# Two chunks of a shared expert behind the routed experts, as seven products of quarters

## The chip, the core and the metric

The kernel runs on one core of one Trainium2 chip, in float32. The metric is the device time of one execution in microseconds (us), from runs of the whole program. A profile is one execution recorded by the hardware; its times count from the span's start.

## What is computed

Input are x (4 batches of 1024 tokens with 1024 channels), a side input of the same size, and weights. Two layers follow each other.

```python
mix(r, k) = sigmoid(r) * num / max(den, 1e-8) * (0.8 + 0.2*tf)   # num, den: forward and backward scans over time
x = x + mix(x, f) @ (w0 * s0).T + b0                              # layer 0
x = x + moe(mix(x, f))                                            # layer 1
# moe(y): h = rmsnorm(y) * nw
#   routed: each token's 4 best of 32 experts, silu(h @ w1[:, :512]) * (h @ w1[:, 512:]) @ w2, weighted sum
#   shared: (silu(h @ sg) * (h @ su)) @ sd,  sg, su, sd of 1024 x 1024
#   result: y + routed + shared
```

The part that matters here is the shared expert: three products of 1024 x 1024 matrices for each of 4096 tokens.

## The kernel before

The tokens are cut into 8 chunks of 512 (q = 0 to 7, two to a batch). A chunk stands in the memory as 8 tiles of 128 channels x 512 tokens. A product of a 1024 x 1024 matrix with a chunk is 8 pieces (one for each 128 output channels); a piece is 8 matmuls of 128 x 128 by 128 x 512 that gather in one bank of PSUM.

**First stage.** VectorE mixes: 64 units, one for each batch, tile of 128 channels and layer; the last three batches hold layer 0 and layer 1 of each tile beside each other. A unit is a forward scan of two halves (L281), a backward scan (L293), and passes (L324, L325, L311, L312, L314 and L315 for layer 0, L317 for layer 1), spread over three steps. ACT does the exponentials and stores a finished unit with a DMA in its own queue (L341). TensorE runs pieces: `first_ffn(q)` (L433, layer 0 of a chunk, then the gate of layer 1 in L467 and its residual in `resT_d`), `shared_up(q)` (L645, 16 pieces: gate and up of the shared expert in turn, L654 multiplies) and `shared_down(q)` (L673, 8 pieces, each followed by 4 transposes in L678 and a store into `sum_d`). `norm_route(q)` (L525 to L616) normalises, chooses the experts and writes rows of h for the experts' gathers.

The order of TensorE's pieces is written out in `order()` (L895 to L921). The order of VectorE against them is planned while the program is built: `run` keeps an account of VectorE's and TensorE's work in microseconds and writes out mixing steps while VectorE's account is below `PACE` (0.9) times TensorE's. Evacuations of a piece are written out one or two pieces later (`after`). `mix_until` writes out all mixing steps that a piece's inputs need. Each engine then runs its own list in order and waits where data are not there. Loads are issued on SP's queue in the order of the list, two pieces ahead; a load that waits holds up those behind it.

The end of that order before:

```python
for b in range(2, B):
    q = NCH * b
    pieces += first_ffn(q, True) + first_ffn(q + 1, True) + shared_down(q - 1)
    pieces += shared_up(q) + shared_down(q)
    if b + 1 < B:
        pieces += shared_up(q + 1)
```

So chunk 7 alone has no shared expert here. During the last 32 pieces the plan of the experts is made (`plan`) and their first weights come in.

**Experts.** 68 units of two blocks of 128 tokens and 12 of one block. A unit of two does its products in the manner of Strassen and Winograd: a product of two matrices cut into quarters takes seven products of quarters instead of eight, and 4 sums of each side and 7 of results. `products` (L1109 to L1152) is that sequence: seven products in three PSUM banks, ACT copies the first, VectorE adds the others. VectorE makes the sums of weights (L838, L858) and of tokens (L984 to L988). Results are added to rows of `sum_d` by an indirect DMA (L1101).

**Tail.** Behind the last unit stands the shared expert of chunk 7: 16 pieces (L1305) with silu and multiplication (L1309, L1310), then 8 pieces (L1329) with bias and residual (L1334). Each 128 x 512 result is turned by 4 transposes (L1315), added to the rows that hold the experts' sums (L1317) and stored (L1318). Its h was kept in `hT_d` by `norm_route(7)` (L530) and is loaded while the last units run (`ahead_1`, `ahead_2`). Seven copies bring the finished chunks from `sum_d` to the output (L1285).

Of the kernel before, what the change touches and what calls it, by code (L numbers as in the profile page):

```python
# [8 lines left out]
FP = mybir.dt.float32  # L9
# [3 lines left out]
ALU = mybir.AluOpType  # L13
# [9 lines left out]
P = 128  # L23
# [8 lines left out]
def kernel(  # L32
# [37 lines left out]

    c0_d = dram.tile([B, NC, P, T], FP, name="c0_d")
    c1_d = dram.tile([B, NC, P, T], FP, name="c1_d")
    hT_d = dram.tile([NC, P, CH], FP, name="hT_d")
    resT_d = dram.tile([NC, P, NT], FP, name="resT_d")

    h_d = dram.tile([NT + P, C], FP, name="h_d")
# [75 lines left out]
    with tc.tile_pool(name="empty", bufs=1) as pz:  # L152
        zeros = pz.tile([P, 2 * C], FP, name="zeros")
        nc.gpsimd.memset(zeros, 0.0)
        nc.sync.dma_start(out=h_d[bass.ts(NT // P, P), :], in_=zeros[:, 0:C])
        nil_i = pz.tile([P, E * BPE // P, BLK], I32, name="nil_i")
        nc.gpsimd.iota(nil_i, pattern=[[0, E * BPE // P], [1, BLK]], base=NT, channel_multiplier=0)
        nil = pz.tile([P, E * BPE // P, BLK, 2], FP, name="nil")
        nc.gpsimd.memset(nil, 0.0)
        nc.gpsimd.tensor_copy(nil[:, :, :, 0], nil_i)  # L160
        nc.sync.dma_start(
            out=slots_d[0 : E * BPE * BLK, :].rearrange("(p r s) o -> p r s o", p=P, s=BLK), in_=nil
        )
        nc.sync.dma_start(
            out=slots_d[E * BPE * BLK :, :].rearrange("(p s) o -> p s o", p=1), in_=nil[0:1, 0, :, :]
        )

        for n in range((NT - CH) // P, NT // P, 2):
            nc.scalar.dma_start(
                out=sum_d[bass.ds(n * P, 2 * P), :].rearrange("(p r) c -> p (r c)", p=P), in_=zeros  # L170
            )
        nc.scalar.dma_start(out=sum_d[bass.ts(NT // P, P), :], in_=zeros[:, 0:C])
# [37 lines left out]
    W_SCANS, W_MIN, W_PASS, W_HALF = 4.7, 0.7, 1.25, 0.75  # L210
    W_PIECE, W_SMALL = 6.9, 1.0
    LATENCY = 12.0
    PACE = 0.9
    table = [None]

    def exp_ln(to, of, func, **kw):
# [152 lines left out]

    beside = []  # L370
    c1s, rTs = {}, {}

    class Piece:

# [29 lines left out]
    def first_ffn(q, gated):  # L404
# [4 lines left out]
        def early(ot):  # L409
            if not gated:  # L410

                nc.sync.dma_start(out=resT_d[ot, :, bass.ts(q, CH)], in_=xT[b, bass.ts(ot, P), cols])
            else:
                xs[ot] = px.tile([P, CH], FP, name="x")
                nc.sync.dma_start(out=xs[ot], in_=xT[b, bass.ts(ot, P), cols])
            if ot == 0:
                mix_until(*((b, ct, 0) for ct in range(NC)))
                if q == 0:
                    work["tensor"] += LATENCY
                for ct in range(NC):  # L420
                    c0s.append(pc0.tile([P, CH], FP, name="c0"))
                    nc.sync.dma_start(out=c0s[ct], in_=c0_d[b, ct, :, cols])
            tiles[ot] = pw0.tile([P, NC, P], FP, name="w0t")
            nc.sync.dma_start(out=tiles[ot], in_=w0[ot])
            if gated:
                mix_until((b, ot, 1))
                c1s[q, ot] = (ph, pc1)[q % NCH].tile([P, CH], FP, name="c1")
                nc.sync.dma_start(out=c1s[q, ot], in_=c1_d[b, ot, :, cols])

        def do(ot):  # L430
# [87 lines left out]
    def norm_route(q):  # L518
# [7 lines left out]
        yield 3.4, 0.0  # L526
        for ct in range(NC):
            nc.vector.scalar_tensor_tensor(hs[ct], hs[ct], v["nw"][:, ct : ct + 1], rs, ALU.mult, ALU.mult)
            if q == NT // CH - 1:
                nc.sync.dma_start(out=hT_d[ct], in_=hs[ct])  # L530
        yield NC * W_HALF, 0.0
        lgT_ps = ps_tr.tile([E, CH], FP, name="tr")
        for ct in range(NC):
# [361 lines left out]
    def order():  # L895
# [18 lines left out]
        pieces += first_ffn(2, True) + first_ffn(3, True) + shared_up(2) + shared_down(2) + shared_up(3)  # L914
        for b in range(2, B):
            q = NCH * b
            pieces += first_ffn(q, True) + first_ffn(q + 1, True) + shared_down(q - 1)
            pieces += shared_up(q) + shared_down(q)
            if b + 1 < B:
                pieces += shared_up(q + 1)  # L920
        return pieces  # L921

    with tc.manual_schedule(engines={PE, DVE, ACT, POOL, SP}):
# [13 lines left out]
    with ExitStack() as m:  # L937
# [220 lines left out]
            for _ in s:  # L1158
                pass

        def run_units(us, loaded, ahead=()):


            if not loaded:
# [40 lines left out]
                held = u  # L1205
            rest_of(held.left)
            rest_of(held.down_sums)
            rest_of(held.down())
            held.add()

# [29 lines left out]

        last = NT // CH - 1
        cols = bass.ts(last, CH)
        end = {}

        def pieces_of(tile):
            flat = tile.rearrange("p k f -> p (k f)")
            n = flat.shape[1] // C
            return [flat[:, bass.ts(i, C)].rearrange("p (k f) -> p k f", f=P) for i in range(n)]  # L1250

        def weights(i):

            to = end["places"][i % len(end["places"])]
            f, n = divmod(i, 2)
            w = (sg, su)[n][:, bass.ts(f, P)] if f < NSI else sd[:, bass.ts(i - 2 * NSI, P)]
            nc.sync.dma_start(out=to, in_=w.rearrange("(k p) f -> p k f", p=P))
            return to

        before_last, last_unit = (len(whole) - 2) % 2, (len(whole) - 1) % 2  # L1260

        def ahead_1():
            one, two = have["w1"][before_last]
            hT = end["hT"] = one.rearrange("p k (h t) -> p (k h) t", t=CH)
            nc.sync.dma_start(out=hT, in_=hT_d.rearrange("k p t -> p k t"))
            end["places"] = pieces_of(two)
            end["wt"] = {i: weights(i) for i in range(4)}

        def ahead_2():
            end["places"] = end["places"] + [x for w in have["w1"][last_unit] for x in pieces_of(w)]  # L1270
            for i in range(4, 12):
                end["wt"][i] = weights(i)

        main = [Unit(u, i % 2) for i, u in enumerate(whole)]
        with tc.manual_schedule(engines=ENG):
# [1 line left out]
                u.load = iter(())  # L1277
            main[0].up_sums = iter(())
            main[0].hs = have["first"]
            run_units(main, True, (ahead_1, ahead_2))  # L1280

            o = have["w2"][before_last]
            nc.sync.dma_start(out=o, in_=sum_d[bass.ts(last, CH), :].rearrange("(t p) c -> p t c", p=P))
            for q in range(last):
                nc.sync.dma_start(out=out[bass.ts(q, CH), :], in_=sum_d[bass.ts(q, CH), :])  # L1285
            acts = [have["t_up"][i][:, k, :] for i in (2, 3) for k in range(NK)]
            rs = [have["t_up"][4][:, k, :] for k in range(NK)]
            banks = [(ps_g, "gA"), (ps_g, "gB"), (ps_g, "gC"), (ps_y, "dA"), (ps_y, "dB"), (ps_y, "dC")]
            used = 0

            def bank():
                nonlocal used
                pool, name = banks[used % len(banks)]
                used += 1
                return pool.tile([P, CH], FP, name=name)

            wt, hT = end["wt"], end["hT"]
            lead = len(end["places"])
            for f in range(NSI):
                gu = []  # L1300
                for n in range(2):
                    i = 2 * f + n
                    mm = bank()
                    for kt in range(NC):
                        nc.tensor.matmul(mm, lhsT=wt[i][:, kt, :], rhs=hT[:, kt, :], start=(kt == 0), stop=(kt == NC - 1))  # L1305
                    gu.append(mm)
                    if i + lead < 2 * NSI + NC:
                        wt[i + lead] = weights(i + lead)
                nc.scalar.activation(acts[f], gu[0], AF.Silu)  # L1309
                nc.vector.tensor_tensor(acts[f], acts[f], gu[1], ALU.mult)  # L1310

            def turned(ct, r):
                rows = ps_t.tile([P, CH // P, P], FP, name="tr")
                for t in range(CH // P):
                    nc.tensor.transpose(rows[:, t, :], r[:, bass.ts(t, P)], ident)  # L1315
                part_o = o[:, :, bass.ts(ct, P)]
                nc.vector.tensor_tensor(part_o, part_o, rows, ALU.add)  # L1317
                nc.scalar.dma_start(  # L1318
                    out=out[cols, bass.ts(ct, P)].rearrange("(t p) c -> p t c", p=P), in_=part_o
                )  # L1320

            held = None
            for ct in range(NC):
                i = 2 * NSI + ct
                r = rs[ct % len(rs)]
                nc.sync.dma_start(out=r, in_=resT_d[ct, :, cols])
                mm = bank()
                for f in range(NSI):
                    nc.tensor.matmul(mm, lhsT=wt[i][:, f, :], rhs=acts[f], start=(f == 0), stop=(f == NSI - 1))  # L1329
                if i + lead < 2 * NSI + NC:  # L1330
                    wt[i + lead] = weights(i + lead)
                if held:
                    turned(*held)
                nc.vector.scalar_tensor_tensor(r, mm, v["b0"][:, ct : ct + 1], r, ALU.add, ALU.add)  # L1334
                held = (ct, r)
            turned(*held)


# [55 lines left out]
```

## Time and profile before

Three runs took 5104.92, 5109.55 and 5104.85 us, median 5104.92. The profiled execution took 5109.81 us with a span of 5107.8 us.

| stretch of the span (us) | what runs | TensorE busy | VectorE busy |
|---|---|---|---|
| 0 to 197 | mixing alone | 0 | nearly full |
| 400 to 1150 | mixing beside pieces | 740.9 of 750 | 625.8 |
| 1150 to 1465 | chunks 4 and 5, mixing of batch 3 | 306.4 of 315 | 255.1 |
| 1465 to 1633 | down of 4, up of 5 | 168.0 of 168 | 32.6 |
| 1633 to 2022 | chunks 6 and 7, routing, plan | nearly full | light |
| 2022 to 4934 | experts | full | about half |
| 4934 to 5108 | shared expert of chunk 7 | nearly full | light |

The profile's columns: engine, line of the kernel, operation, output and inputs, count; in a timeline the first two numbers are start and duration in us, and brackets give the idle time before it and what ended that. PE is TensorE's matmul, PEld its weight load, DVE VectorE, ACT ScalarE, POOL GpSimd, SP the engine that issues loads. A float32 matmul appears as two passes, so 8 matmuls count x16. Matmul durations overlap; the distance of starts is their pace.

### The profile page before, as it was taken

To read this page: it belongs to the slowest core of one execution; us is meant where nothing else is said; L and a number is where in the kernel's file an instruction comes from. 1 tells how busy PE (TensorE), PEld (TensorE's weight loads), DVE (VectorE), ACT (ScalarE), POOL (GpSimd) and SP (SyncE) were. 2 spreads that over 40 slices of the span, in tenths; PEclk is the share of its full clock that TensorE was granted. 3 is DMA by queue.
4 is the path that set the end of the run, shared out by engine and by line. 5 is a ranking of instruction groups with operands and counts; after the bars stand their busy time and mean duration, and the time that the engine had idled before them with its cause. 6 is when DMAs were issued, how large, how long until landed. Compare 5 with 4: busy or idle time off the path is not lost.

```text
span 5107.8 us, 36503 instructions
## 1 busy us (share of the span) xinstructions
PE 4823.9 (94%) x12906; PEld 2235.0 (44%) x12906; DVE 3130.7 (61%) x3280; ACT 1445.5 (28%) x1840; POOL 818.4 (16%) x765
## 2 busy tenths in 40 slices
PE   0479999999999998999999999999999999999999
PEld 0124444444444443444444444444444444444444
DVE  9988887887860222656565656556565656565621
ACT  5557656566540210111111111111111111111110
POOL 0113202302310220111111111111111111111110
PEclk9989999999999999999999999999999999999999
DMA  4678679669754845676767676767676777777784
GB/s 139 192 206 216 181 222 269 174 198 277 194 160 127 236 128 189 214 233 220 233 216 241 212 241 212 241 214 239 214 239 214 239 229 224 229 224 229 224 233 118
DMA packets 524212, 1077.77 MB, mean 211 GB/s; under 512 B 30642, under 2 KB 260147, under 8 KB 523411
## 3 DMA queue, kind: packets, MB, share of 16 engines
q1 hardware_dynamic: 386338, 744.70, 42.9%
q0 software_dynamic: 74656, 223.12, 20.9%
q10 hardware_dynamic: 63024, 107.50, 6.0%
q8 instruction: 105, 1.72, 0.1%
q14 instruction: 89, 0.72, 0.0%
HBM read 844.13 MB, written 203.56 MB: 205 GB/s over the span
## 4 chain that ended last, share of the span: by engine, by line
PE 60%; ACT 0%; issue 0%; DVE 0%; ACTq 0%
PE gA L1117 14%; PE gC L1117 9%; PE gB L1117 9%; PE dA L1117 7%; PE dB L1117 5%; PE dC L1117 5%; PE tr L971 2%; PE gA L1005 2%; PE gB L1005 2%; PE tr L1054 1%; PE dA L1067 1%; PE dB L1067 1%; PE gB L1305 0%; PE gC L1305 0%; PE gA L1305 0%; PE dA L1305 0%
## 5 line engine op out<-in xcount | busy, mean ns | idle before, releaser
L645 PE MATMUL mm<-c,wpc 128*128 128x512 f32 x1792 | 777.7, 593 | 0.9 <-DMA wpc<-in_su 0.9
L433 PE MATMUL mm<-c,w0t 128*128 128x512 f32 x1024 | 447.9, 599 | 213.9 <-DMA w0t<-in_w 212.4
L645 PEld LDWEIGHTS mm<-c,wpc 128*128 128x128 f32 x1792 | 337.9, 190 | 416.1 <-issue 412.5
L1117 PE MATMUL gA<-w,hsT 128*128 128x512 f32 x1088 | 489.6, 593 | 0.0
L1117 PE MATMUL gC<-w,s_up 128*128 128x512 f32 x1088 | 489.1, 592 | 0.0
L1117 PE MATMUL gB<-t_up,s_up 128*128 128x512 f32 x1088 | 489.1, 592 | 0.0
L1101 POOL DMA_INDIRECT sum_d<-y,tokens x148 | 306.3, 2070 | 917.2 <-DMA sum_d<-y,tokens 541.8
L871 POOL DMA_INDIRECT hs<-h_d,tokens x146 | 147.7, 1012 | 1621.8 <-PE tr L971 1540.3
L433 PEld LDWEIGHTS mm<-c,w0t 128*128 128x128 f32 x1024 | 196.2, 192 | 461.8 <-issue 456.4
L673 PE MATMUL mm<-sact,wpc 128*128 128x512 f32 x896 | 395.2, 596 | 0.0
L1117 PEld LDWEIGHTS gB<-t_up,s_up 128*128 128x128 f32 x1088 | 206.7, 190 | 260.2 <-issue 244.2
L1117 PEld LDWEIGHTS gC<-w,s_up 128*128 128x128 f32 x1088 | 206.7, 190 | 260.2 <-issue 260.2
L838 DVE TENSOR_TENSOR t_up<-w,w 128x2048 f32<-128x2048 f32 x136 | 310.7, 2285 | 0.0
L1117 PEld LDWEIGHTS gA<-w,hsT 128*128 128x128 f32 x1088 | 201.7, 190 | 227.8 <-issue 227.8
L293 DVE TENSOR_TENSOR_SCAN fg<-decay,tail,fg 128x1024 f32<-128x1024 f32 x128 | 292.9, 2330 | 0.0
L1117 PE MATMUL dB<-t_down,s_down 128*128 128x512 f32 x544 | 256.9, 595 | 0.1
L1117 PE MATMUL dA<-w,actT 128*128 128x512 f32 x544 | 255.8, 592 | 0.0
L1117 PE MATMUL dC<-w,s_down 128*128 128x512 f32 x544 | 255.8, 592 | 0.0
L972 ACT COPY hsT<-tr 128x512 f32<-128x512 f32 x296 | 172.7, 588 | 291.8 <-PE tr L971 291.8
L673 PEld LDWEIGHTS mm<-sact,wpc 128*128 128x128 f32 x896 | 168.1, 191 | 198.2 <-issue 196.7
L1117 PE MATMUL gA<-t_up,hsT 128*128 128x512 f32 x544 | 244.5, 592 | 0.0
L1042 ACT ACTIVATE act<-c 128x512 f32<-128x512 f32 x68 | 42.8, 630 | 708.9 <-DVE c L1038 708.9
(245 smaller groups left out, 6210.8 us busy)
## 6 DMA issues: line engine op xcount, KB each, us to landing
w<-in_w SPq DMA_DIRECT2D x240, 2048.0 KB, 9.1
fg<-euk POOLq DMA_DIRECT2D x64, 512.0 KB, 6.5
c_d<-r ACTq DMA_DIRECT2D x64, 512.0 KB, 7.9
c<-c_d SPq DMA_DIRECT2D x128, 256.0 KB, 6.8
w0t<-in_w SPq DMA_DIRECT2D x64, 512.0 KB, 6.4
wpc<-in_sg SPq DMA_DIRECT2D x56, 512.0 KB, 5.0
wpc<-in_su SPq DMA_DIRECT2D x56, 512.0 KB, 5.0
wpc<-in_sd SPq DMA_DIRECT2D x56, 512.0 KB, 5.4
```

The source lines that it names most:

```text
L293: nc.vector.tensor_tensor_scan(fg[:, m, ::-1], decay[L][:, ct, b : b + 1].to_broadcast([P, T]), fg[:, m, ::-1], tail[:, m : m + 1], ALU.mu ...
L433: nc.tensor.matmul(mm, lhsT=tiles[ot][:, it, :], rhs=c0s[it], start=(it == 0), stop=(it == NC - 1))
L645: nc.tensor.matmul(mm, lhsT=wts[f, n][:, kt, :], rhs=c1s[q, kt], start=(kt == 0), stop=(kt == NC - 1))
L673: nc.tensor.matmul(mm, lhsT=wts[ct][:, f, :], rhs=acts[q, f], start=(f == 0), stop=(f == NSI - 1))
L838: nc.vector.tensor_tensor(to, x, y, ALU.subtract)
L871: nc.gpsimd.indirect_dma_start(out=to, out_offset=None, in_=h_d, in_offset=bass.IndirectOffsetOnAxis(ap=have["tokens"][:, i, n : n + 1], a ...
L971: nc.tensor.transpose(tr[:, r, :], hs[:, bass.ts(4 * q + r, P)], ident)
L972: nc.scalar.copy(self.hsT[:, 4 * q : 4 * q + 4, b, :], tr)
L1005: nc.tensor.matmul(ps, lhsT=self.hsT[:, k, 0, :], rhs=w[k // NK][:, k % NK, bass.ts(n, I)], start=(k == 0), stop=(k == NC - 1),)
L1067: nc.tensor.matmul(ps, lhsT=self.actT[:, k, 0, :], rhs=w[:, k, bass.ts(n, 512)], start=(k == 0), stop=(k == NI - 1),)
L1101: nc.gpsimd.indirect_dma_start(out=sum_d, out_offset=bass.IndirectOffsetOnAxis(ap=tokens[:, i, self.n : self.n + 1], axis=0), in_=y, in_of ...
L1117: nc.tensor.matmul(ps, lhsT=x[:, k, :], rhs=w[:, k, :], start=(k == 0 and not more), stop=(k == half - 1), skip_group_check=more,)
```

## The change

The shared expert of chunk 6 leaves the first stage, and stands with that of chunk 7 in the tail, where the two chunks side by side (1024 tokens) are multiplied in seven products of quarters. The order becomes:

```diff
-            pieces += first_ffn(q, True) + first_ffn(q + 1, True) + shared_down(q - 1)
-            pieces += shared_up(q) + shared_down(q)
+            pieces += first_ffn(q, True) + first_ffn(q + 1, True)
             if b + 1 < B:
-                pieces += shared_up(q + 1)
+                pieces += shared_down(q - 1) + shared_up(q)
+            else:
+                pieces += shared_down(q - 2) + shared_up(q - 1) + shared_down(q - 1)
```

Ahead of chunk 6's first layer 24 pieces are gone (down of 4, up of 5), and the 32 behind chunk 7 are down of 4, up of 5, down of 5. Since chunk 5's tiles are still held then, chunk 7's gate tiles lie in two buffers of the mixing (`fg`). `PACE` becomes 0.93. `hT_d` holds two chunks, so chunk 6's h is stored too (8 DMAs more on SP's queue), and the zeros for `sum_d` cover one chunk more (two DMAs of 1 MB more on ACT's queue at the start).

The tail is new. `weights(i)` loads two tiles of 128 columns, one of each half of the matrix; unit i of 0 to 7 is gate or up (in turn) of output tiles m and m + 4, units 8 to 11 are down. Each unit makes four sums of its weights, and seven products of four matmuls:

```diff
+        def weight_sums(i):
...
+            nc.vector.tensor_tensor(s[1], a21, a22, ALU.add)
+            nc.vector.tensor_tensor(s[2], s[1], a11, ALU.subtract)
+            yield
+            nc.vector.tensor_tensor(s[3], a11, a21, ALU.subtract)
+            nc.vector.tensor_tensor(s[4], a12, s[2], ALU.subtract)
+            yield
...
+        def chunk_sums(quarters, t):
+            (b11, b12), (b21, b22) = quarters
+            for to, x, y in ((t[3], b22, b12), (b12, b12, b11), (t[2], b22, b12), (t[4], b21, t[2])):
+                nc.vector.tensor_tensor(to, x, y, ALU.subtract)
+                yield
...
+            for i in range(NSI):
+                m = i // 2
+                if 0 < i and i + 3 < NSI + HF:
+                    weights(i + 3)
+                nxt = weight_sums(i + 1)
+                take = take_up(m) if i % 2 else take_gate(m)
+                for n, _ in enumerate(unit_of(i, h_quarters, have["t_up"], HF, take)):
+                    if n < 4:
+                        next(done, None)
+                    elif n < 6:
+                        next(nxt, None)
+                rest_of(done)
+                rest_of(nxt)
+                done = act_sums(m) if i % 2 else iter(())
+                if i < tail:
+                    nc.sync.dma_start(out=out[bass.ts(i, CH), :], in_=sum_d[bass.ts(i, CH), :])
```

The sums of the two chunks' h (four of 128 x 2048) are made once, in `begin_tail`, which `run_units` calls behind the last token sums and ahead of the last unit's down product; the sums of the activations (four of 128 x 512) are made after each up unit. `take_gate` and `take_up` add, apply silu and multiply per quarter. The four down units add bias and residual and turn each result as before, 16 in all. The first weights go to token buffers and to the weights of the last unit of two; three units ahead are under way at a time. The copies to the output are six, one after each of the first six units.

## The prediction

> **What bounds the kernel now.** First the page's shares of busy time and its slices:
>
> ```profile
> PE 4823.9 (94%) x12906; PEld 2235.0 (44%) x12906; DVE 3130.7 (61%) x3280; ACT 1445.5 (28%) x1840; POOL 818.4 (16%) x765
> PE   0479999999999998999999999999999999999999
> DVE  9988887887860222656565656556565656565621
> ```
>
> From the fourth slice TensorE (PE) is busy nearly throughout; VectorE (DVE) is near full only in the first twelve slices, where the mixing runs beside the matmuls. Two places matter: the end of the mixing, where the change takes matmuls away, and the tail, where it puts them back. The first, in TensorE's timeline (start, length; each matmul shows as two passes):
>
> ```profile
> 1150.29 55.10 PE L433 MATMUL mm<-c,w0t 128*128 128x512 f32 x128
> 1213.50 43.49 PE L433 MATMUL mm<-c,w0t 128*128 128x512 f32 x96 [8.11 <-DMA w0t<-in_w]
> ...
> 1464.78 20.76 PE L673 MATMUL mm<-sact,wpc 128*128 128x512 f32 x48
> ...
> 1633.10 55.10 PE L433 MATMUL mm<-c,w0t 128*128 128x512 f32 x128
> ```
>
> 1150.29 is the first layer's product of chunk 4, 1633.10 that of chunk 6. At 1464.78 the up products of chunk 4 are over; from there to 1633.10 stand the 24 pieces that the change takes out of this place. When the mixing ends, in VectorE's timeline:
>
> ```profile
> 1465.05 0.69 DVE L654 TENSOR_TENSOR sact<-sact,mm 128x512 f32<-128x512 f32 x1 [8.33 <-PE mm L645]
> ...
> 1482.67 1.23 DVE L315 TENSOR_TENSOR r<-r,xg 128x1024 f32<-128x1024 f32 x1 [1.50 <-ACT xg L224]
> ...
> 1493.57 1.23 DVE L317 TENSOR_TENSOR r<-r,fg 128x1024 f32<-128x1024 f32 x1 [0.52 <-DMA fg<-euk]
> ```
>
> L315 at 1482.67 finishes the last layer-0 unit of batch 3, which chunk 6 needs; L317 the last of all. VectorE here waits for TensorE (8.33 us before L654): the mixing ends at 1494 because its steps stand behind products, not because VectorE is full. Last the tail:
>
> ```profile
> 4933.53 7.03 PE L1305 MATMUL gA<-w,w 128*128 128x512 f32 x16
> ...
> 5057.13 0.60 PE L1315 MATMUL tr<-ident,t_up 128*128 128x128 f32 x4
> 5057.57 7.03 PE L1329 MATMUL gA<-t_up,w 128*128 128x512 f32 x16
> ...
> 5100.97 0.60 PE L1315 MATMUL tr<-ident,t_up 128*128 128x128 f32 x4
> 5103.10 0.63 PE L1315 MATMUL tr<-ident,t_up 128*128 128x128 f32 x4 [1.53 <-DVE t_up L1334]
> ```
>
> From 4933.53 the 24 pieces of chunk 7 follow each other every 6.87 us without a gap; the last ends at 5100.97, and 6.83 us later the span is over.
>
> **The change, part by part.** A piece is 8 matmuls and takes 6.867 us from start to start, so one matmul 0.858 us. A group of four transposes takes 0.44.
>
> *Taken from the first stage:* 1633.10 - 1464.78 = 168.3 us (24 x 6.867 = 164.8, and 8 transpose groups, 3.5). What follows chunk 7's first layer keeps its shape, 8 down, 16 up and 8 down pieces (of chunks 4 and 5 in place of 5 and 6), so routing and plan have the same cover of 32 pieces.
>
> *Put into the tail:* 8 up and 4 down units of 7 products of 4 matmuls: 336 matmuls, where the two chunks took 384. 336 x 0.858 = 288.4; 15 of the 16 transpose groups on the path, 6.6; the end as now with one more VectorE add ahead of it, 6.83 + 0.69 = 7.5. Tail 302.5, before 174.3 (4933.53 to the span's end 5107.8): +128.2.
>
> [...] The row decides: pieces start exactly 6.87 us apart with the next one's operands there, so 48 x 0.858 = 41.2 us go.
>
> *Does the mixing end in time?* Without the 24 pieces chunk 6 could begin at 1464.8. In the new order on VectorE the last layer-0 unit of batch 3 stands behind the product of the fifth gate (L654's place) of chunk 4, the last layer-1 unit behind the sixth; in the old one they stand behind the first and second down piece after the next chunk's up. The fifth product ends six pieces before 1464.8, at 1423.6. Then L654 0.7, two scans 4.5, four passes 4.9: 1433.7. In the trace the store of the 1482.67 result is issued at 1489.48, 5.6 us after its end, and such stores land in 5.3 to 9.2 us: 1444.6 to 1448.5. The load on SP takes 6.6 to 8.7, with the weight tile close behind it: 1452 to 1458. That is 7 to 13 us before 1464.8, so no wait, if VectorE keeps up. From the first product of chunk 4 (1157.2) to the fifth gate it has 20 forward and 20 backward scans (2.3 us each), eleven units' L324 and L325 (2.4 a unit), ten units' L311 and L312 (2.4), L314 with L315 (2.5) or L317 (1.2), 9 of new keys, 61 half passes of 0.74, two reciprocals of 3.4 and 11 of routing: some 234 us in 266, 88%. In this stretch it now runs at 255 of 315 (81%), in its fullest 50 us at 47.05 (94%). It must also have come 1.7 units (some 28 us) further by 1157, which the planner's 0.93 in place of 0.9 asks of it; between 400 and 1150 it was idle for 124 of 750 us. So it keeps up with little to spare: I take 0, bounds 0 and +37 (mixing as late as now: data at 1502). A gain is excluded, since the pieces are already counted out in full.
>
> *Small edits at nothing, and their cover.* Two more 1 MB stores of zeros on ACT's queue at 10 us: ACT idles 9.65 us after, and the next k load, issued at 21.31, is needed at 34.04, when 5 us more of traffic (390 to 420 GB/s there) have passed; without cover up to 5. Eight more stores of normed rows on SP wait for VectorE's norm, with the down weights queued behind; chunk 7 does this now with no gap on TensorE; up to 5. Chunk 6's gate tiles now wait on SP until the last up piece of chunk 4 has used its tiles, with the second weight tile (6.7 us to land) queued behind; the wait ends 6 us before chunk 6 begins and the tile is needed 6.87 us after it. Six copies of sums to the output, one per unit, for seven at once, and 1 MB of weights per 24 us, asked for three units ahead: some 5 MB per 24 us, 210 GB/s, where the tail now moves 340 in its fullest 50 us.
>
> *The new chain into the tail.* VectorE is free at 4926.1 (last y). Two weight sums of 0.69 and three chunk sums of 2.29 (the L838 row, 128x2048) put the third sum's result at 4934.4; the second product needs it at 4933.5 + 3.4 = 4937.0. The chunks' loads start at 4879 and 4886, the first weights at about 4899. Covered by 2.6 us; without cover the whole 12 us of sums. I take 1.
>
> *VectorE inside the tail.* Of 24.0 us per unit a gate takes 9 operations of 0.69, an up unit 17, a down unit 13 and four of 0.75: 6 to 12 us. The experts' stage runs this same helper with 0.0 idle before its matmuls. Taken as 0, upper bound one 1.4 us handover per unit, 17; below nothing is excluded.
>
> Sum: -168.3 + 128.2 + 1 = -39.1. The profiled execution took 5109.8 us (span 5107.8 and 2.0 around it), giving 5070.7. It lies 4.9 above the median 5104.92 and next to the highest of the three; against the median the sum gives 5066.
>
> **Rivals.**
> 1. *The mixing comes late* and TensorE waits at chunk 6, by 10 to 37 us: 5076 to 5103, say 5088. For it: VectorE's 88%, and routing steps that wait up to 9.9 us for small products. Against: the 7 to 13 us of margin. 8%.
> 2. *Handovers in the tail show*, up to 17 us, or the 12 us of first sums: about 5080. Against: the experts' 0.0. 7%.
> 3. *Slower.* Place: chunk 6's first product; mechanism: with the 24 pieces gone, the same mixing has to fit in 168 us less matmul time, and VectorE becomes the bound there. The gain is gone when the wait passes 39 us, and it is slower by 0.2% (about what a measurement can tell from no change, 10 us) from a wait of 49: the last layer-0 unit would have to end after 1494, later than now, so VectorE would do its 234 us in 327, 72%, under the 81% it shows. Priced at 55 us: 5121. 3%.
> 4. *The matmuls are not saved* because products of four need more time each than pieces of eight: the order shows 336 in place of 384, and the experts' products of 8 passes start 3.43 us apart, the same 0.43 per pass. [...] 2%.
>
> **How the numbers follow.** The forecast's own case, 80%, is 5066 with 5058 to 5075 around it (the 4.9 us between the runs, small edits up to 5). 8 in 10 would be met by that; since the upper ends of rivals 1 and 2 are real I reach to 5088. Faster by over 0.2% (below 5094.7) takes the forecast's case, rivals 2 and 4 and half or more of 1: 0.93. Within 0.2%: the late part of 1, 0.04. Slower: 0.03.
>
> **What would show it.** Right: chunk 6's first product starts near 1465 with no wait on c loads; the experts start near 1854 in place of 2022.42; the tail is about 302 us with products 3.43 us apart. Wrong: a wait before chunk 6's products or a gap between products in the tail. The prediction falls if VectorE lags behind the products of chunks 4 and 5, and the waits there are for VectorE.

## The result and the profile after

| | before | after |
|---|---|---|
| median of 20 runs each | 5106.49 us (5101.79 to 5111.55) | 5095.67 us (5090.31 to 5104.23) |
| ratio | 1 | 0.998, 95% interval 0.9973 to 0.9987 |
| profiled execution, span | 5109.81, 5107.8 us | 5095.89, 5093.8 us |

The kernel became 0.2% faster: 10.8 us by the medians, a little over a quarter of the 39 us that the prediction summed up. In the changed kernel the lines of the first stage stand some 7 lower down: L433 is now L440, L645 L652, L673 L680, L678 L685, L819 L826. The page after, busy time first and then the slices:

```profile
PE 4793.8 (94%) x12810; PEld 2220.2 (44%) x12810; DVE 3225.9 (63%) x3416; ACT 1434.3 (28%) x1833; POOL 811.1 (16%) x765
PE   0479999999899979999999999999999999999999
DVE  9988988888752226565656565565656565656434
```

TensorE's busy time is 30 us less, but the span only 14 us shorter. In TensorE's row the eleventh slice (1273 to 1401 us) is now 8, where it was 9, and the one in which the experts begin is 7, where it was 8. TensorE's timeline at the same places as in the prediction, with its new waits between them:

```profile
1150.46 55.10 PE L440 MATMUL mm<-c,w0t 128*128 128x512 f32 x128
1209.09 43.13 PE L440 MATMUL mm<-c,w0t 128*128 128x512 f32 x96 [3.53 <-DMA w0t<-in_w]
...
1302.16 1.12 PE L685 MATMUL tr<-ident,rT 128*128 128x128 f32 x4 [6.17 <-ACT hr L554]
1306.97 1.12 PE L552 MATMUL tr<-ident,c 128*128 128x128 f32 x4 [2.71 <-ACT rT L686]
...
1377.72 1.11 PE L552 MATMUL tr<-ident,c 128*128 128x128 f32 x4 [4.71 <-ACT rT L686]
...
1478.77 55.10 PE L440 MATMUL mm<-c,w0t 128*128 128x512 f32 x128
...
1807.39 8.69 PE L680 MATMUL mm<-sact,wpc 128*128 128x512 f32 x16 [12.18 <-DMA wpc<-in_sd]
...
1881.22 3.78 PE L980 MATMUL tr<-ident,t_down 128*128 128x128 f32 x16 [11.46 <-DVEq L1243]
...
4792.48 3.60 PE L1126 MATMUL gA<-w,hs 128*128 128x512 f32 x8
...
5088.84 0.63 PE L1461 MATMUL tr<-ident,t_up 128*128 128x128 f32 x4 [1.22 <-DVE t_up L1475]
```

The waits of 3.53 and 11.46 us are not new (8.11 and 11.59 before). Read the rest by stretches. The tail (4792.48 to 5093.8) is 301.3 us, the experts (1881.22 to 4792.48) 2911.3 as before (2911.1). Chunk 6's first product begins at 1478.77, not 1465, and the experts at 1881.22, not 1854. So all 27 us that are missing lie ahead of the experts: the stretch from chunk 4's first product to the end of its up products grew from 314.5 to 328.3 (+13.8), and that from chunk 6's first product to the experts from 389.3 to 402.5 (+13.1).

**Loss one, ahead of chunk 6.** There is no wait for chunk 6's data at 1478.77. TensorE waits earlier, in the routing of chunks 4 and 5, and for ScalarE. ScalarE's timeline after:

```profile
1267.27 0.71 ACT L224 ACTIVATE y<-x,v_b 128x512 f32<-128x512 f32 x1
1280.70 0.57 ACT L543 COPY hr<-tr 32x512 f32<-32x512 f32 x1 [12.73 <-PE tr L541]
1281.30 1.28 ACT L219 ACT_TABLE_LOAD   x1
1282.59 1.06 ACT L220 ACTIVATE ek<-ek 128x1024 f32<-128x1024 f32 x1
...
1297.23 1.06 ACT L224 ACTIVATE xg<-xg 128x1024 f32<-128x1024 f32 x1 [4.40 <-DMA xg<-in_xT]
...
1301.54 0.56 ACT L554 COPY hr<-tr 128x512 f32<-128x512 f32 x1
```

and VectorE's:

```profile
1267.52 0.68 DVE L253 TENSOR_SCALAR ek<-k 128x1024 f32<-128x1024 f32 x1
...
1270.63 1.22 DVE L317 TENSOR_TENSOR r<-r,fg 128x1024 f32<-128x1024 f32 x1
1283.68 1.23 DVE L259 TENSOR_TENSOR ekv<-ek,k 128x1024 f32<-128x1024 f32 x1 [11.82 <-ACT ek L220]
```

VectorE has the input of the exponential `ek` ready at 1268.2. ScalarE does `ek` at 1282.59, because in its queue `ek` stands behind the copy of chunk 4's router logits (L543), and that copy waits 12.73 us for logits whose matmuls (L541) stand on TensorE behind a product. VectorE idles 11.82 us for `ek`; the mixing steps are then late, and with them what ScalarE does for them. One of these, the sigmoid of `xg`, waits 4.40 us more for its load, which ScalarE issued only behind the late exponentials. Behind all of this stand the copies of turned rows (L554 at 1301.54), whose PSUM banks TensorE needs at 1302.16. So a wait for TensorE came back to TensorE by way of two other queues. In the kernel before the same copy waited 11.07 us, and no `ek` stood behind it:

```profile
1285.47 0.57 ACT L536 COPY hr<-tr 32x512 f32<-32x512 f32 x1 [11.07 <-PE tr L534]
...
1286.35 1.06 ACT L224 ACTIVATE xg<-xg 128x1024 f32<-128x1024 f32 x1 [0.30 <-issue]
```

Nothing passed the waiting copy: ScalarE ran nothing from 1267.98 to 1280.70, and `ek` came 14.4 us after its input.

The windows' view of the stretch from the end of chunk 5's first layer to the end of chunk 4's up products (length; busy PE, PEld, DVE, ACT, POOL; granted clock, DMA share, GB/s), before:

```profile
1271.40:1464.80 193.40, 192.92 (x532) 87.99 (x531) 158.69 (x169) 111.81 (x118) 60.94 (x78) 1.00 0.66 178
```

and after:

```profile
1266.70:1478.80 212.10, 198.27 (x532) 90.45 (x531) 154.41 (x168) 109.44 (x116) 61.74 (x81) 0.96 0.68 185
```

The same 532 matmuls took 18.7 us more: TensorE's idle time grew from 0.5 to 13.8 us, and 5.4 us went to slower matmuls (busy 198.27 for 192.92), with a granted clock of 0.96 in place of 1.00 (the four transposes after each wait take 1.12 us where they take 0.66 elsewhere). VectorE was busy 154 of 212 us, 73%: it was not full. The stall at 1209.09, ahead of this stretch, gave 4.6 us back (3.53 in place of 8.11).

**Loss two, behind chunk 7's first layer.** SP's timeline (issues of loads) after:

```profile
1771.82 0.37 SPq L673 DMA_DIRECT2D wpc<-in_sd  x1
1787.05 1.00 SPq L826 DMA_DIRECT2D w<-in_w  x2
1788.09 0.51 SPq L673 DMA_DIRECT2D wpc<-in_sd  x1
1788.79 12.65 SPq L833 DMA_DIRECT2D w<-in_w  x1
1801.48 0.51 SPq L673 DMA_DIRECT2D wpc<-in_sd  x1
```

and its waits there (in total, times, longest):

```profile
SPq L826 <- PE mm L652: 13.5, 1, 13.5
```

Before, the same load was issued 1.7 us behind the first tile of down weights:

```profile
1925.59 0.37 SPq L666 DMA_DIRECT2D wpc<-in_sd  x1
1927.27 0.97 SPq L819 DMA_DIRECT2D w<-in_w  x2
```

L826 (L819 before) loads the first expert's weights. The tiles stand where the stack of pools was that `plan` closes, and one of those pools, `pc1`, holds chunk 5. Before, the up products in this place were chunk 6's, whose tiles lie in `ph`, outside that stack; now they are chunk 5's. So the load waits until the last of them has been read, and the second tile of down weights (issued in L673 of the changed kernel) queues behind it and behind two transfers of 2 MB that start only then: the product that needs it starts 19.3 us after its issue at 1788.09, with 12.18 us of waiting, at 1807.39.

### The profile page after: what moved, and what is told of

Read it like the earlier page. It is cut to its first block, busy times and chain, and to the rows that moved or that the text cites. A ratio compares the mean times of both kernels' runs of the same rounds, so it can differ in the third digit from the quotient of the medians.

```text
span 5093.8 us, 36409 instructions
## 1 busy us (share of the span) xinstructions
PE 4793.8 (94%) x12810; PEld 2220.2 (44%) x12810; DVE 3225.9 (63%) x3416; ACT 1434.3 (28%) x1833; POOL 811.1 (16%) x765
## 4 chain that ended last, share of the span: by engine, by line
PE 63%; ACT 0%; issue 0%; DVE 0%; ACTq 0%
PE gA L1126 15%; PE gC L1126 10%; PE gB L1126 10%; PE dA L1126 8%; PE dB L1126 5%; PE dC L1126 5%; PE tr L980 2%; PE gA L1014 2%; PE gB L1014 2%; PE tr L1063 1%; PE dA L1076 1%; PE dB L1076 1%; ACT hsT L981 0%; PE tr L1461 0%; ACT y L1083 0%
## 5 line engine op out<-in xcount | busy, mean ns | idle before, releaser
L652 PE MATMUL mm<-c,wpc 128*128 128x512 f32 x1536 | 667.1, 593 | 0.0
L440 PE MATMUL mm<-c,w0t 128*128 128x512 f32 x1024 | 450.0, 601 | 206.7 <-DMA w0t<-in_w 206.7
L1126 PE MATMUL gC<-w,s_up 128*128 128x512 f32 x1184 | 532.3, 592 | 0.0
L1126 PE MATMUL gB<-t_up,s_up 128*128 128x512 f32 x1152 | 517.9, 592 | 0.0
L652 PEld LDWEIGHTS mm<-c,wpc 128*128 128x128 f32 x1536 | 289.6, 190 | 355.1 <-issue 353.9
L440 PEld LDWEIGHTS mm<-c,w0t 128*128 128x128 f32 x1024 | 196.7, 193 | 456.1 <-issue 444.5
L680 PE MATMUL mm<-sact,wpc 128*128 128x512 f32 x768 | 345.3, 604 | 14.9 <-DMA wpc<-in_sd 12.2
L1126 PEld LDWEIGHTS gC<-w,s_up 128*128 128x128 f32 x1184 | 224.8, 190 | 282.2 <-issue 282.2
L1126 PEld LDWEIGHTS gB<-t_up,s_up 128*128 128x128 f32 x1152 | 218.9, 190 | 275.5 <-issue 259.5
L680 PEld LDWEIGHTS mm<-sact,wpc 128*128 128x128 f32 x768 | 146.3, 195 | 189.0 <-issue 185.0
```

The source lines that it names most:

```text
L440: nc.tensor.matmul(mm, lhsT=tiles[ot][:, it, :], rhs=c0s[it], start=(it == 0), stop=(it == NC - 1))
L652: nc.tensor.matmul(mm, lhsT=wts[f, n][:, kt, :], rhs=c1s[q, kt], start=(kt == 0), stop=(kt == NC - 1))
L680: nc.tensor.matmul(mm, lhsT=wts[ct][:, f, :], rhs=acts[q, f], start=(f == 0), stop=(f == NSI - 1))
L1126: nc.tensor.matmul(ps, lhsT=x[:, k, :], rhs=w[:, k, :], start=(k == 0 and not more), stop=(k == half - 1), skip_group_check=more,)
```

## The experiments

All compare with the kernel before on the same chip; its median there was 5106.5 to 5109.0 us. "First" is the stretch from chunk 4's first product to the end of its up products (to chunk 6's first product where the order is the new one), "second" from chunk 6's first product to the experts, both from the profiled execution. "Copy" is that of the router logits, "pools" those of even and odd chunks.

| kernel | median us | ratio, 95% interval | first | second |
|---|---|---|---|---|
| before | 5106.5 to 5109.0 | 1 | 314.5 | 389.3 |
| after | 5095.67 | 0.998 (0.9973 to 0.9987) | 328.3 | 402.5 |
| before, PACE 0.93 | 5124.14 | 1.0034 (1.0022 to 1.0046) | 327.8 | 386.8 |
| after, PACE 0.9 | 5104.28 | 0.9992 (0.9985 to 0.9999) | 337.2 | 403.3 |
| after, pools changed over | 5081.18 | 0.9949 (0.9935 to 0.9962) | 327.7 | 387.8 |
| after, copy later for 4 | 5084.88 | 0.9953 (0.994 to 0.9967) | 318.9 | 400.1 |
| after, copy later for 4, 5 | 5075.21 | 0.9934 (0.992 to 0.9947) | 311.1 | 400.2 |
| pools, copy for 4 | 5074.64 | 0.9932 (0.9919 to 0.9946) | 317.5 | 390.4 |
| pools, copy for 4, 5 | 5066.20 | 0.9916 (0.9903 to 0.993) | 310.8 | 389.2 |
| pools, copy for all | 5070.99 | 0.9926 (0.9912 to 0.9939) | 315.4 | 389.2 |
| pools, copy for 4, PACE 0.92 | 5077.26 | 0.9944 (0.9931 to 0.9958) | 318.4 | 389.7 |
| after, direct products in the tail | 5134.64 | 1.006 (1.0045 to 1.0076) | | |

**The tail's own saving.** The seven products undone in the tail: direct products, without the sums of weights, of chunks and of products, and with the turns of results at other steps of a unit. The rest is as after, and part of the edit is shown:

```diff
-            dict(zip("1234567", zip((a11, a12, s[4], a22, s[1], s[2], s[3]), (b11, b21, b22, t[4], t1, t[2], t[3])))),
+            for n, which in enumerate(("11", "22", "21", "12")):
+                r, c = int(which[0]) - 1, int(which[1]) - 1
...
+                for h in range(2):
+                    for k in range(half):
+                        nc.tensor.matmul(
+                            ps,
+                            lhsT=w[r][:, h * half + k, :],
+                            rhs=quarters[h][c][:, k, :],
+                            start=(h == 0 and k == 0),
+                            stop=(h == 1 and k == half - 1),
+                        )
```

> The changed kernel with the seven products of quarters undone in the tail alone: each of its 12 steps makes its four outputs from 32 direct matmuls in place of 28, and the sums of weights, of chunks and of products are left out. The tail of both chunks stays behind the experts. Theory (TensorE's matmuls set the tail, 0.858 us each): 12 x 4 x 0.858 = 41.2 us more, tail 301.3 + 41 = 342 us, 5137 us, slower than the kernel before. Rival (the sums on VectorE or the shortened overlap hold the tail as it is, so that direct products give back part): under 30 us more. Second rival (the weight-load rows, not the matmul rows, set the tail): 18 us more, 5114 us.

```profile
4788.60 7.03 PE L1319 MATMUL gA<-w,hs 128*128 128x512 f32 x16
...
5125.35 0.66 PE L1444 MATMUL tr<-ident,t_up 128*128 128x128 f32 x4 [0.41 <-DVE t_up L1458]
```

The tail takes 5130.4 - 4788.6 = 341.8 us, 40.5 more than with seven products. That is the 41.2 of the matmul row, not the 18 of the weight-load row (96 loads for the 48 matmuls, 190 ns each at L645 in the profile before), and none of it is given back by leaving out the sums.

**Where loss one comes from.** One number of the kernel before:

```diff
-    PACE = 0.9
+    PACE = 0.93
```

> The kernel before with PACE 0.93 in place of 0.9 and nothing else. Theory (the faster pace is what puts ek behind chunk 4's copy of the logits, whatever comes after): the stretch from chunk 4's first layer to the next chunk's grows by up to 14 us of the 18.7 us seen, less the 4.6 us that the stall at chunk 5 shrinks: 5110 to 5120 us. Rival (the new order, not the pace, makes the collision): 5100 to 5107 us.

TensorE's timeline of this kernel (its lines are those of before):

```profile
1303.81 1.12 PE L678 MATMUL tr<-ident,rT 128*128 128x128 f32 x4 [5.90 <-ACT hr L547]
1308.63 1.12 PE L545 MATMUL tr<-ident,c 128*128 128x128 f32 x4 [2.71 <-ACT rT L679]
...
1378.74 1.11 PE L545 MATMUL tr<-ident,c 128*128 128x128 f32 x4 [4.76 <-ACT rT L679]
...
1481.12 19.05 PE L673 MATMUL mm<-sact,wpc 128*128 128x512 f32 x44
```

The three waits of after stand here to within 0.3 us, ScalarE's copy of the logits waits 12.73 us for TensorE and `ek` follows it as there, and the first stretch, from 1153.34, is 327.8 against 328.3. So the new pace makes loss one, whatever is moved behind it. The stretch grew by 13.3 us with the shorter stall at chunk 5 counted in, where the theory had at most 14 less 4.6: the loss is larger than expected, and the time of 5124.1 us is 4 us above the theory's range, still further from the rival's. The kernel is 17 us slower by the medians, 13.4 us by the spans (5121.2 and 5107.8). And the reverse, the changed kernel with the old pace:

```diff
-    PACE = 0.93
+    PACE = 0.9
```

> The changed kernel with PACE 0.9 in place of 0.93, the kernel before's value, and nothing else. Theory (the place of the steps against one another decides, not the rate as such): the collision at chunk 4's routing falls elsewhere, and by the plan's own count mixing of the last pair ends at most some us later: 5080 to 5094 us. Rival (the higher pace is needed because the mixing has 24 pieces fewer to lie beside): chunk 6 waits for its data, up to 37 us, 5100 to 5130 us. Second rival (the rate 0.93 is the whole of the loss before chunk 6): 5081 to 5083 us with the first product of chunk 6 near 1465.

```profile
1487.84 57.03 PE L440 MATMUL mm<-c,w0t 128*128 128x512 f32 x128 [22.46 <-issue]
```

The waits in the routing are gone, and chunk 6 waits 22.5 us. SP's timeline at its eight loads, and VectorE's at the last layer-0 unit of batch 3:

```profile
1445.85 36.69 SPq L423 DMA_DIRECT2D c<-c_d  x8
```

```profile
1470.83 1.23 DVE L315 TENSOR_TENSOR r<-r,xg 128x1024 f32<-128x1024 f32 x1
```

The loads take SP from 1445.9 to 1482.5, and the unit ends at 1472.1: so the wait is read as one for late mixing, though the trace names no releaser for it. The time, 5104.3 us, is in the range of the first rival, that the higher pace is needed. So the prediction's rival of a late mixing, 10 to 37 us, was right about this pace. Neither rate is free: 0.93 costs 13 to 14 us in the first stretch, 0.9 costs 22.5.

**Loss two undone.** The pools of even and odd chunks changed over, so that chunk 5 lies outside the closed stack; every engine's list stays the same, only what the loads wait for changes:

```diff
-                    c1s[q, ot] = (ph, pc1)[q % NCH].tile([P, CH], FP, name="c1")
+                    c1s[q, ot] = (pc1, ph)[q % NCH].tile([P, CH], FP, name="c1")
```

> The changed kernel with one edit: the chunks of even number take the tiles of the pool pc1 and those of odd number the tiles of ph, the other way round from now. Chunk 5 then lies in ph, outside the stack of pools that the plan closes, so the first expert weights on SP no longer wait for TensorE's last product of shared_up(5); the order of instructions on every engine is otherwise the same. Theory (the wait of 13.5 us in SP's queue is what made the down weights 12.2 us late): that gap goes, the expert stage starts 11 to 13 us earlier, near 1869, and the kernel takes about 5083 us. Rival (the two transfers of 2 MB take the transfer engines ahead of the down weights in any case): the gap stays or moves, 5092 to 5097 us.

SP's timeline of this kernel:

```profile
1767.85 0.37 SPq L673 DMA_DIRECT2D wpc<-in_sd  x1
1769.52 0.98 SPq L826 DMA_DIRECT2D w<-in_w  x2
1775.22 0.38 SPq L673 DMA_DIRECT2D wpc<-in_sd  x1
```

The expert's weights are issued 1.7 us behind the first down tile, where it was 15.2; no down piece waits for its weights, and the second stretch is 14.7 us shorter (387.8). The experts start at 1863.1, earlier than the 1869 expected, of which 2.9 us come from an earlier start of chunk 4. By the medians' ratios the gain is 0.31% or 16 us, and 5081.2 us is 2 us below the forecast. The two transfers as such cost nothing, so that rival falls.

**Loss one undone.** The copy of the logits is written out one piece later:

```diff
+        if q == 4:
+            yield 0.0, 0.0
         nc.scalar.copy(lgT, lgT_ps)
```

> The changed kernel with one edit: for chunk 4 alone, the copy of the router logits on ScalarE is issued one piece later than their matmuls, so that the exponential ek of the next mixing row stands before it in ScalarE's queue and not behind it. Theory (ek was held behind a copy that waited 12.7 us for TensorE, which idled VectorE 11.8 us and then TensorE 13.6 us and its clock): chunk 6's first product begins near 1465 in place of 1478.8, and the kernel takes 5081 to 5087 us. Rival (VectorE or ScalarE is simply too full in this stretch, and the wait comes back a few us on): first product 1475 or later, 5092 to 5098 us.

The wait of 6.17 us is gone and the first stretch 9.4 us shorter; 4.77 us in chunk 5's routing stay. First product of chunk 6 at 1474.4, from a start that was 5 us later than after's. The time, 5084.9 us, is in the theory's range, but this product lies between the two expectations; the wait in chunk 5's routing has to be taken with it. Both mends together, for chunk 4 first:

> The changed kernel with both edits, chunk 5 in the pool outside the closed stack and chunk 4's copy of the logits one piece later. Theory (two separate losses of about 14 and 12.5 us): they add up, the expert stage starts at 1853 to 1858 and the kernel takes 5067 to 5073 us. Rival (one cause behind both, or one gives the other's time back): no better than the better of the two alone, 5081 us or more.

They add up in the stretches (317.5 and 390.4), but the experts start at 1861.6 and the time is 5074.6 us, 4 and 2 us above the theory's ranges. Then the same line with `if q in (4, 5)`:

> Chunk 5 in the pool outside the closed stack, and the copy of the router logits one piece later for chunks 4 and 5. Beside the run with chunk 4 alone (span 5073.9, where TensorE still waits 4.6 us for ScalarE in chunk 5's routing and has 0.93 of its clock after it), theory (chunk 5's copy holds ScalarE's queue in the same way): that wait and the dip go, 5 to 7 us less, 5066 to 5070 us. Rival (there the queue is held by the sigmoid that waits for its row by transfer, and by the length of the ScalarE work itself): within 2 us of 5074.

ScalarE's timeline of this kernel at chunk 4's routing:

```profile
1271.57 1.06 ACT L220 ACTIVATE ek<-ek 128x1024 f32<-128x1024 f32 x1
...
1282.99 0.57 ACT L545 COPY hr<-tr 32x512 f32<-32x512 f32 x1 [5.48 <-PE tr L541]
```

and TensorE's:

```profile
1299.31 0.65 PE L554 MATMUL tr<-ident,c 128*128 128x128 f32 x4 [1.04 <-ACT rT L688]
...
1463.57 55.10 PE L440 MATMUL mm<-c,w0t 128*128 128x512 f32 x128
...
1852.74 3.78 PE L982 MATMUL tr<-ident,t_down 128*128 128x128 f32 x16 [11.23 <-DVEq L1245]
```

`ek` now stands ahead of the copy, VectorE waits no more for it, and TensorE's largest wait between 1256 and 1463 is 1.04 us. Chunk 6 begins near 1465 and the experts near 1854, as the prediction had it, and the kernel takes 5066.2 us. That is in the theory's range, and faster than both kernels. Without the changed pools, to see whether the two are separate:

> The changed kernel with the copy of the router logits one piece later for chunks 4 and 5, and the pools as they are. Theory (two separate losses that add up: with the other pool as well it took 5066 us, the pool alone 5081): this gives 5078 to 5083 us, first product of chunk 6 near 1464, and the gap of 12 us before the down piece behind chunk 7's first layer stays. Rival (the gain of the later copy came only together with the other pool): 5086 us or more.

First stretch 311.1, second 400.2: the one mend shortens the first stretch alone, by 17 us of the 18.7 that waits and slower matmuls had cost there, and the wait for the down weights stays at 12.6 us. The median is 3 us below the range expected. And the later copy for every chunk (no condition on q):

> Chunk 5 outside the closed stack, and the copy of the router logits one piece later for all chunks, where the run before had it for 4 and 5 alone. Theory (the later copy frees ScalarE's queue wherever mixing steps stand beside routing, chunks 0 to 5): the same or a little faster than 5066 us, 5060 to 5068 us, with no wait of TensorE for ScalarE's copies over 2 us between 400 and 1480. Rival (any shift of the steps deals the collisions anew, and the run for 4 and 5 was a lucky deal): 5070 us or more, with other waits in place of those that are gone.

Slower than with chunks 4 and 5 alone by 0.1%, which the intervals don't separate, with a wait of 2.92 us for a copy at 1309 and one of 4.58 for a weight tile at 789 in place of others. The theory is missed, and the rival's terms are met: 5071.0 us, with other waits in place of those that are gone. So the later copy is no remedy everywhere, and how much of the 5066.2 us is a lucky order of the steps is not known; that the waits at the routing of chunks 4 and 5 go with their copies is what the two kernels with these two copies alone show (first stretch 311.1 and 310.8). Last, a pace between:

```diff
-    PACE = 0.93
+    PACE = 0.92
```

> Both edits (chunk 5 outside the closed stack, chunk 4's copy one piece later) with PACE 0.92. At 0.93 the mixing's last rows are done before chunk 6 needs them and VectorE is nearly idle from 1450 on; at 0.9 chunk 6 waits 22.5 us. Theory (the end of the mixing moves evenly with PACE): at 0.92 it is about 7 us later than at 0.93, where some slack is left, so chunk 6 waits 0 to 7 us: 5072 to 5082 us, and the places of the collisions change. Rival (the order around chunk 5's routing happens to fall better): 5066 to 5070 us.

Chunk 6 waits 1.5 us, within the theory's 0 to 7, and the waits in the routing lie elsewhere (2.40 us at 1313.64); 5077.3 us is in the theory's range too. The first stretch is 318.4 in place of 317.5 us. So the pace between brings no better deal.

## Why the prediction was wrong, point by point

- **24 pieces out, -168.3 us.** Right as a sum: with both losses mended the experts start at 1852.7, 169.7 us earlier than before. The changed kernel itself got 141.2. In the 169.7 us stand 3.7 from a shorter first stretch and a start of chunk 4 that is 2.5 later; neither was foreseen, and they nearly cancel.
- **The tail, 302.5 us.** Right: 301.3, products 3.43 us apart. The seam into it was taken at 1 us and shows at 0.15.
- **48 matmuls fewer, 41.2 us.** Right: the direct products, which put them back, take 40.5 us more.
- **"So it keeps up with little to spare: I take 0, bounds 0 and +37".** This step failed, in mechanism and place. It weighed VectorE's busy time (88%) and looked for the price at chunk 6's first product. There the wait is indeed 0. In the kernel with both mends, where chunk 6 begins at 1463.57, the last layer-0 unit ended at 1442.7 and not at 1433.7, so some 9 of the 7 to 13 us of margin were used. But the step also priced at nothing what the planner's 0.93 "asks of it". The pace alone costs 13.3 us in the first stretch of the kernel before, and by the same waits 13.8 in the changed one, because it puts an exponential of the mixing behind a ScalarE copy that waits for TensorE. VectorE was only 73% busy meanwhile. The prediction had named the place as a sign of being wrong, the products of chunks 4 and 5, but the engine was another: TensorE's waits there are for ScalarE's copies, not for VectorE. A sum of busy times cannot show this; the lists of ScalarE before and after, read side by side at the routing, could have.
- **"What follows chunk 7's first layer keeps its shape ... so routing and plan have the same cover of 32 pieces".** This step failed too, by 13.1 us. The shape of TensorE's list is the same, but its operands are other tiles: chunk 5's, in a pool that the plan closes. The prediction listed what queues on SP for the moved stores and gate tiles, and left out the expert's first load, whose wait had changed.
- **Small edits at nothing.** No gap stands at the stores of h, the gate tiles of chunk 6 or the zeros. The stall at chunk 5's first layer shrank by 4.6 us, which the prediction had not counted.
- **The rivals.** The late mixing is real at the old pace (22.5 us) and was bought off by the new one. The measured 5095.67 lies in that rival's 5076 to 5103, but not by its mechanism, as chunk 6 does not wait. Handovers in the tail did not show (the 1.4 us for one was the author's estimate; TensorE's one wait of the tail is 1.22 us, ahead of the last transposes), nor did a slower kernel. That matmuls go unsaved, which the chances count among the faster cases, no run shows: the 48 put back took 40.5 us.

The sum: 13.8 and 13.1 us lost ahead of the experts against some 2 us better in tail and seam make the 25 us between the forecast of -39.1 and the -13.9 of the profiled executions. That the losses are these two and separate is shown by the mends. Open is what the 5.4 us of lower clock would be worth by themselves; they came and went with the waits, and no run separates them. The mends of ScalarE's queue also move other steps by a piece, so their exact size is that of these lists.

## What to carry to other kernels

When a change moves work or a planner's rate, compare the lists of every engine, also the lightly loaded ones: here ScalarE, busy for 28% of the span, brought TensorE's idle time in a stretch from 0.5 to 13.8 us, because copies that waited 12.73 and 6.40 us for TensorE stood ahead of work for the mixing. When pieces change places with others of equal size, ask of each which buffers it holds and until when, and which load takes over that space. A gain that is sure on the bounding engine is worth what is left after these two.

## What the runs showed of the hardware

In the changed kernel, after waits of 6.17, 2.71 and 4.71 us, the next four transposes took 1.11 to 1.12 us where they take 0.66. The granted clock was 0.88 in the 50 us slice of the first two (1300 to 1350) and 0.97 in that of the third (1350 to 1400), where the kernel before had 1.00 in both; 13.8 us of waits (0.5 before) and 5.4 us of longer matmuls make the stretch 18.7 us longer. With the changed pools and the later copies for chunks 4 and 5, where these waits are gone, both slices have 1.00. Waits of about 2 us do not sort by length. Two waits for a weight tile in the changed kernel, with six pieces behind each:

```profile
788.99 43.13 PE L440 MATMUL mm<-c,w0t 128*128 128x512 f32 x96 [2.04 <-DMA w0t<-in_w]
...
1535.90 41.44 PE L440 MATMUL mm<-c,w0t 128*128 128x512 f32 x96 [2.03 <-DMA w0t<-in_w]
```

The granted clock was 0.72 in the 6 us behind the first and 1.00 behind the second; the six pieces behind the first took 1.7 us longer. Which of the shorter waits go with a lower clock is not settled here.
